# A list scheduler that chooses its plan by replays with varied times, in a fused fp32 attention, channel-mix and state-space kernel

## The chip, the cores and the metric

The kernel runs on one core of a Trainium2 chip, in float32 throughout. The metric is the device time of one execution in microseconds: the median over the runs of one kernel. A core has five engines with instruction queues of their own: TensorE (PE in the profile, its weight loads PEld), VectorE (DVE), ScalarE (ACT), GpSimd (POOL) and SyncE (SP), which here only issues transfers. Each works through its queue in order, and an instruction that waits for another engine holds up everything behind it in its own queue. So the order in which a program is written out, engine by engine, decides what waits for what.

## The reference

The input is X, 4 batches of 1024 tokens of 256 features. Four layers follow one another, each adding its result to x; LN is a layer norm over the features without weights.

```python
x = x + attention(LN(x))          # causal, one head of 256: softmax(Q K^T / 16) V
x = x + mix(LN(x))                # channel mix
x = x + states(LN(x))             # state space, 16 states
x = x + mix(LN(x))                # channel mix, the same weights

def mix(x):
    x_prev = shift(x, 1)          # the token before, 0 for the first
    xr = mu_r * x + (1 - mu_r) * x_prev
    xk = mu_k * x + (1 - mu_k) * x_prev
    return sigmoid(xr @ W_r.T) * (relu(xk @ W_k.T) ** 2 @ W_v.T)

def states(x):                    # has a layer norm of its own, with ln_g and ln_b
    x_proj, z = split((LN(x) * ln_g + ln_b) @ W_in.T + b_in)
    B_proj = x_proj @ W_B.T * mean(dt)
    y = causal_convolution(B_proj, mean over d of A_bar ** t) @ W_C.T + D_skip * x_proj
    return (y * silu(z)) @ W_out.T + b_out + x
```

The output is the last x.

## The kernel before

x stays in SBUF, 32 tiles of 128 tokens (eight to a batch). Work goes by half batches of 512 tokens, numbered 0 to 7; most operations on VectorE, ScalarE and GpSimd are 128 partitions by 512 floats. Operands of TensorE with the features on the partitions come from the rows by a detour through DRAM: normalised rows are written out (`.w`), read back in blocks (`.r0` to `.r3`), and turned by VectorE within 32 by 32 blocks (L731).

Every piece of work has a name, and the prediction uses these. The letter in front is the layer: `a` attention, `f` the first channel mix, `h`, `s`, `z` and `y` the state layer, `g` the second channel mix; then the half batch. `a6.st0` to `st3` are the statistics of the four tiles of half batch 6 (L603 and L604, VectorE), `.ve`, `.rs`, `.mrs` the small powers and shifts (L629, L642 on GpSimd, L651), `.xn0` to `.xn3` the normalised rows (L657 on VectorE or L663 on ScalarE), `a6.xa0` and `a6.xa1` the turned columns. `a1.q1` is a copy of queries out of PSUM. For a batch `qs2`, `qs3` are the query products, done in the manner of Strassen and Winograd with seven products `p1` to `p7` of blocks in place of eight: `T1` to `T4` are sums of inputs (L813), `u1` a copy out of PSUM, `u2`, `u3`, `c11` to `c22`, `v12` sums of outputs (L838). `gks0` to `gks3` and `zs0` to `zs3` do the same for the second mix's keys and the state layer's gates. `p22` is the masked maximum of tile 22's scores with its copy out of PSUM (L1502 and L1508), `v23` tile 23's values (L1474), `pT` a turned probability block (L1550), `a.x18` the addition of tile 18's attention into x. In a mix `xr0`, `xr1`, `xk0`, `xk1` are the mixed operands (L927 on ScalarE, L930 on VectorE), `pr0`, `pr1` the gate products into PSUM (L881), `g0`, `g1` their sigmoid (L1016), `relu`, `ka` the keys (L987 and L988), `pv` the value products, `rv` their product with the gate (L1038, VectorE), `x0`, `x1` the addition into x (L1044, GpSimd). `y0.6` and the like multiply z with the state layer's output (L1903), `pyo` are that layer's output products.

No scheduler of the language orders this program: it is scheduled by hand, by the class `Order`. While the kernel is described, `op` logs an operation with its needs and one or several ways to do it (an engine and an assumed time; an engine written as `DVE+port` shares a port with GpSimd), `unit` logs a group of matmuls, whose order on TensorE is that of the description, and `take` and `known` log a PSUM tile taken and a time given. PSUM is two pools, four tiles `bank` and two `pair`; a group takes the tile that came free first, by the model.

`finish` then plans. `_due` gives each operation a time at which it must be done for TensorE never to wait. For each of 20 plans, `_run` simulates the program: when an engine is free it takes, among the operations that could start within WAIT of the first, the one due soonest; a way is chosen by its modelled end; SHARE and MARGIN hold an operation back by a part of its slack. Each plan is run five times (ROUNDS): after each run the operations that a TensorE group waited for are made due earlier (`_hurry`), by the wait. The run with the lowest modelled end, with its due times, is run again, and this time writes the instructions. Assumed times are such as `dve(n)`, 0.02 + n/850 us, or 1.27 for an addition of 512 columns on GpSimd; a transfer lands at the queue's modelled end plus LANDING, 0.24.

Of the kernel before, what the change touches and what calls it, by code (L numbers as in the profile page):

```python
# [4 lines left out]

# [47 lines left out]
class Order:  # L53
# [23 lines left out]
        for share, margin in ((0.2, 2.5), (0.1, 1.5), (0.3, 4.0), (0.2, 1.5), (0.1, 2.5))  # L77
        for wait in (0.0, 0.08, 0.15, 0.22)
    ]
    ROUNDS = 5  # L80
    TRIALS = 4
    BANKS = {"bank": 4, "pair": 2}
# [95 lines left out]
    def finish(self):  # L178
        dues = self._due()
        self.made = {e["key"]: n for n, e in enumerate(self.log) if e["key"] is not None}  # L180
        self.ends = []
        best = math.inf
        for plan in self.PLANS:
            self.due = list(dues)
            for k in range(self.ROUNDS):
                used = list(self.due)
                end = self._run(plan, False)
                self.ends.append((end, k, plan))
                if end < best:
                    best, chosen = end, (plan, used)  # L190
                for key, wait in self.waits:
                    self._hurry(key, wait)
        plan, self.due = chosen
        self._run(plan, True)

    def _hurry(self, key, wait):

        n = self.made[key]
        while self.log[n]["kind"] == "op":
            self.due[n] -= wait  # L200
            needs = self.log[n]["needs"]
            if not needs:
                return
            n = self.made[max(needs, key=lambda k: self.ready[k])]

    def _run(self, plan, emits):
        self.SHARE, self.MARGIN, self.WAIT = plan
        self.emits = emits
        self.waits = []
        self.now = self.at = 0.0  # L210
        self.free, self.ready, self.offered = {}, {}, []
        self.queue = self.port = 0.0
        self.waiting = {}
        self.psum = {kind: [0.0] * k for kind, k in self.BANKS.items()}
        for n, e in enumerate(self.log):
            if e["kind"] == "op":
                self._enter(n)
            elif e["kind"] == "known":
                self._done(e["key"], e["time"])
            elif e["kind"] == "take":  # L220
                heapq.heappop(self.psum[e["takes"]])
            else:
                self._unit(e)
        while self.offered:
            self._step()
        return max(self.now, *self.free.values())
# [57 lines left out]
    def _step(self):  # L284
        self.at, k = self._first()
        time, n = self.offered.pop(k)
        e = self.log[n]
        end, _, engine, emit = self._way(time, n)
        engine, _, port = engine.partition("+")
        self.free[engine] = end  # L290
        if port or engine == "POOL":
            self.port = end
        if self.emits:
            emit()
        if e["frees"]:
            heapq.heappush(self.psum[e["frees"]], end + self.LAG)
        if e["moves"]:
            for k, work in enumerate(e["moves"]):
                issued = end - (len(e["moves"]) - 1 - k) * self.log[n]["cost"] / len(e["moves"])
                self.queue = max(self.queue, issued + self.FLIGHT) + work  # L300
            self._done(e["key"], self.queue + self.LANDING)
        else:
            self._done(e["key"], end + e["lag"])
# [46 lines left out]
def hybrid_kernel(  # L350
# [548 lines left out]
    class Mix:  # L899
# [1329 lines left out]
```

## Time and profile before

| what | value |
|---|---|
| time of the runs | 465.42 us median (465.42, 465.47, 465.42) |
| the profiled execution's own time | 465.0 us |
| its span | 463.1 us |
| TensorE busy | 456.0 us, 98% of the span |
| VectorE busy | 390.2 us, 84% |
| ScalarE busy | 220.8 us, 48% |
| GpSimd busy | 143.1 us, 31% |
| share of the last-ending chain | PE 86%, DVE 8%, issue 2%, DMA, POOL and ACT 1% each |
| HBM traffic | 149 GB/s over the span |

The span runs from the first to the last recorded instruction of the profiled execution; 1.9 us of that execution lie outside it. A row of a timeline is: start, length in us, engine, line, operation, output and input, number of instructions joined in the row; in brackets, the idle time of that engine before it and what ended it. Rows of one engine may overlap a little, since the next instruction begins while the last one ends. L numbers are lines of the kernel before.

### The profile page before, as it was taken

The page shows a single profiled execution, that of the slowest core. Times are in us where ns is not written, and L with a number is a line of the kernel's source. Part 1 is how long each engine was busy: PE and PEld are TensorE (multiplying, and loading weights), DVE is VectorE, ACT ScalarE, POOL GpSimd, SP SyncE. Part 2 cuts the span into 40 slices and gives each one's busy share as a digit, 9 for nine tenths or more (in the row PEclk, how much of TensorE's full clock was granted, in tenths as well). Part 3 has the DMA queues.
Part 4 walks back from the last instruction along what each step waited for, and adds up shares of the span by engine and source line. Part 5 has one row for each costly group of instructions (what it writes and reads, how often), then busy time and mean ns, then how long its engine had stood idle before and what let it go on. Part 6 is the DMA issues. An engine that isn't in the chain of part 4 may idle for free.

```text
span 463.1 us, 6634 instructions
## 1 busy us (share of the span) xinstructions
PE 456.0 (98%) x2052; PEld 312.5 (67%) x2052; DVE 390.2 (84%) x931; ACT 220.8 (48%) x463; POOL 143.1 (31%) x149
## 2 busy tenths in 40 slices
PE   8999999999999999999999999999999999999996
PEld 5766785667786667786777775474565758675875
DVE  3687769899969999889999977459889999999962
ACT  3422414454342433333556567441458777664652
POOL 3000102112013213121271354962052616826340
PEclk9999999999999999999999999999999999999999
DMA  8047876848455763427866989603022024252442
GB/s 242 21 127 203 250 190 168 222 132 258 117 135 139 221 194 93 118 62 237 224 177 182 275 268 271 260 17 88 11 92 91 1 86 144 81 147 99 129 144 84
DMA packets 84915, 69.44 MB, mean 150 GB/s; under 512 B 20160, under 2 KB 82576, under 8 KB 84880
## 3 DMA queue, kind: packets, MB, share of 16 engines
q1 hardware_dynamic: 84064, 68.76, 50.8%
q10 hardware_dynamic: 816, 0.26, 0.2%
q8 instruction: 16, 0.26, 0.2%
q14 instruction: 19, 0.16, 0.1%
HBM read 40.54 MB, written 28.45 MB: 149 GB/s over the span
## 4 chain that ended last, share of the span: by engine, by line
PE 86%; DVE 8%; issue 2%; DMA 1%; POOL 1%; ACT 1%; SPq 0%; DVEq 0%; POOLq 0%
PE po L1597 13%; PE sc L1492 13%; PE pv L1464 5%; PE p_zs L830 4%; PE p_ss L830 4%; PE p_qs L830 2%; PE p_gks L830 2%; PE py L1848 2%; PE pc L1798 2%; PE dust L1282 1%; DMA blocks_a<-rows_a 1%; PE pr_g0.pr L881 1%; PE pb L1735 1%; PE pp_a0.pq L774 1%; PE pr_g0.pv L881 1%
## 5 line engine op out<-in xcount | busy, mean ns | idle before, releaser
L1597 PE MATMUL po<-v,prT 128*128 128x256 f32 x288 | 67.7, 380 | 0.1
L1492 PE MATMUL sc<-xa,q 128*128 128x512 f32 (+3 forms) x192 | 67.0, 486 | 0.0
L1597 PEld LDWEIGHTS po<-v,prT 128*128 128x128 f32 x288 | 54.2, 189 | 11.6 <-issue 2.6
L1513 ACT ACTIVATE pr<-pr,nmx 128x128 f32<-128x128 f32 (+7 forms) x32 | 24.7, 773 | 64.6 <-DVE pr L1508 57.7
L1492 PEld LDWEIGHTS sc<-xa,q 128*128 128x128 f32 x192 | 35.1, 190 | 24.5 <-issue 19.6
L1464 PE MATMUL pv<-wv,xa 128*128 128x257 f32 x128 | 32.9, 380 | 0.0
L642 POOL TENSOR_TENSOR rs_a<-ve_a,minus_half 128x4 f32<-128x4 f32 x7 | 7.1, 1010 | 76.8 <-DVE ve_a L629 76.8
L1044 POOL TENSOR_TENSOR x<-x,r_f 128x512 f32<-128x512 f32 x16 | 20.3, 1271 | 33.0 <-DVE r_f L1038 32.5
L642 POOL TENSOR_TENSOR rs_h<-ve_h,minus_half 128x8 f32<-128x8 f32 x8 | 13.2, 1647 | 52.5 <-DVE ve_h L631 52.5
L1464 PEld LDWEIGHTS pv<-wv,xa 128*128 128x128 f32 x128 | 23.6, 191 | 7.8 <-issue 3.6
L1508 DVE TENSOR_SCALAR_CACHE_REDUCE pr<-sc,v 128x128 f32<-128x128 f32 (+7 forms) x32 | 26.2, 818 | 1.1
L1550 DVE STREAM_TRANSPOSE prT<-pblocks 128x384 f32<-128x384 f32 (+7 forms) x30 | 23.8, 793 | 2.4 <-DMA pblocks<-exps 2.3
L642 POOL TENSOR_TENSOR rs_f<-ve_f,minus_half 128x4 f32<-128x4 f32 x8 | 8.4, 1053 | 47.1 <-DVE ve_f L629 28.8
L1044 POOL TENSOR_TENSOR x<-x,r_g 128x512 f32<-128x512 f32 x14 | 18.9, 1371 | 11.0 <-DVE r_g L1038 11.0
L1641 POOL TENSOR_TENSOR x<-x,bout_r 128x512 f32<-128x512 f32 x16 | 20.0, 1279 | 4.5 <-ACT x L1634 4.5
L1606 DVE SCALAR_TENSOR_TENSOR x<-po,rsm,x 128x256 f32<-128x256 f32 x32 | 15.0, 470 | 4.3 <-PE po L1597 3.8
L1474 DVE TENSOR_TENSOR v<-pv,bv_r 128x257 f32<-128x257 f32 x32 | 13.4, 418 | 5.6 <-PE pv L1464 5.6
L930 DVE SCALAR_TENSOR_TENSOR xr_g<-hT_g,mur,xr_g 128x512 f32<-128x512 f32 x16 | 17.3, 1112 | 0.0
L663 ACT ACTIVATE xn_f<-x,mrs_f,rs_f 128x256 f32<-128x256 f32 x18 | 9.8, 592 | 15.5 <-DVE mrs_f L651 15.5
L1634 ACT ACTIVATE x<-x,mrs_h,rs 128x256 f32<-128x256 f32 x32 | 16.9, 592 | 0.0
L1903 POOL TENSOR_TENSOR z<-z,skip 128x512 f32<-128x512 f32 x9 | 13.1, 1462 | 10.9 <-DVE skip L1899 10.7
L663 ACT ACTIVATE xn_g<-x,mrs_g,rs_g 128x256 f32<-128x256 f32 x23 | 12.4, 589 | 8.3 <-DVE mrs_g L626 6.7
(458 smaller groups left out, 1089.8 us busy)
## 6 DMA issues: line engine op xcount, KB each, us to landing
hk<-r_dram SPq DMA_DIRECT2D x16, 512.0 KB, 9.2
rows_g<-xn_g SPq DMA_DIRECT2D x8, 512.0 KB, 2.9
blocks_g<-rows_g SPq DMA_DIRECT2D x32, 128.0 KB, 2.8
x<-in_L_attn_a_X_dram SPq DMA_DIRECT2D x7, 512.0 KB, 4.9
rows_f<-xn_f SPq DMA_DIRECT2D x7, 512.0 KB, 3.0
blocks_f<-rows_f SPq DMA_DIRECT2D x28, 128.0 KB, 2.7
rows_h<-xn_h SPq DMA_DIRECT2D x7, 512.0 KB, 3.7
blocks_h<-rows_h SPq DMA_DIRECT2D x28, 128.0 KB, 3.2
```

The lines of the kernel that those rows point to most:

```text
L642: nc.gpsimd.tensor_tensor(rs()[:, :k].rearrange("p k n -> p (k n)"), ve()[:, :k].rearrange("p k n -> p (k n)"), minus_half[:, : k * NH], A ...
L663: nc.scalar.activation(place(n), split(row(n)), AF.Identity, bias=mrs()[:, k - 1, n : n + 1], scale=rs()[:, k - 1, n : n + 1],)
L830: lambda: nc.tensor.matmul(p(), lhsT=w(), rhs=data(), start=True, stop=True), "bank",
L930: nc.vector.scalar_tensor_tensor(t()[:, c, :], hT()[:, c, :HALF], mu1[:, c : c + 1], t()[:, c, :], ALU.mult, ALU.add,)
L1044: nc.gpsimd.tensor_add(xg, xg, r()[:, ts(g, 2), :])
L1464: nc.tensor.matmul(pv()[:, : D + 1], lhsT=xaj()[:, c, ts(n, P)], rhs=wv[:, c, :], start=(c == 0), stop=(c == KC - 1),)
L1492: nc.tensor.matmul(sc()[:, k * HALF : k * HALF + w], lhsT=qh()[:, c, ts(n, P)], rhs=keys[k]()[:, c, :w], start=(c == 0), stop=(c == KC - 1),)
L1508: nc.vector.tensor_scalar(dst, src, v[2 * b + h]()[:, n, D : D + 1], None, ALU.add, ALU.min, accum_out=nmx(),)
L1513: nc.scalar.activation(p()[:, :nk], p()[:, :nk], AF.Exp, bias=nmx(), scale=-1.0, accum_out=sm())
L1550: nc.vector.transpose(dst()[:, : NH * width].rearrange("p (k m a) -> p k m a", m=NH, a=GRP), blocks().rearrange("p m (k a) -> p k m a", a= ...
L1597: nc.tensor.matmul(po()[:, :D], lhsT=src()[:, ts(n, P)], rhs=v[2 * b + n // NH]()[:, n % NH, :D], start=(n == 0), stop=(n == t),)
L1641: nc.gpsimd.tensor_add(xg, xg, bout_r.unsqueeze(1).to_broadcast([P, 2, D]))
```

## The change

`finish` still runs all plans and rounds, but judges each run by `_replays`, the mean end of six replays. A replay goes through the order that the run recorded in `self.trail`, with the engines it chose, and keeps both. Operation times are stretched at random, VectorE's by up to 3%, ScalarE's by up to 4%, GpSimd's by up to 25%, and a transfer lands up to 0.6 us later; TensorE's times stay. What is hurried for the next round is also new: in place of what TensorE waited for in the run, it is what TensorE waited for in the replays, by the mean wait, if that is over 0.1 us. No operation, no assumed time and no arithmetic is edited. The chosen plan and due times differ, and with them the order on each engine, the engine of some operations, and the PSUM tiles.

```diff
@@ class Order
+    SAMPLES = 6
+    SPREAD = {"DVE": 0.03, "ACT": 0.04, "POOL": 0.25}
+    LATE = 0.6
@@ finish
                 used = list(self.due)
-                end = self._run(plan, False)
+                self._run(plan, False)
+                end = self._replays()
                 self.ends.append((end, k, plan))
@@
+    def _replays(self):
+        lost, ends = {}, 0.0
+        for k in range(self.SAMPLES):
+            rng = random.Random(k)
+            ends += self._replay(rng, lost)
+        self.waits = [(key, t / self.SAMPLES) for key, t in lost.items() if t > 0.1 * self.SAMPLES]
+        return ends / self.SAMPLES
+
+    def _replay(self, rng, lost):
+        now = queue = port = 0.0
+        free, ready = {}, {}
+        psum = {kind: [0.0] * k for kind, k in self.BANKS.items()}
+        for n, way in self.trail:
+            e = self.log[n]
...
+            if e["kind"] == "unit":
+                for _ in range(e["many"] if e["takes"] else 0):
+                    at = max(at, heapq.heappop(psum[e["takes"]]))
+                if last is not None and at > now + 0.1:
+                    lost[last] = lost.get(last, 0.0) + at - now
+                now = max(now, at) + e["cost"]
+                ready[e["key"]] = now + self.LAG
+                continue
+            engine, shared, cost = way
+            if e["moves"]:
+                at = max(at, queue - self.FLIGHT - 0.5)
+            at = max(at, free.get(engine, 0.0), port if shared or engine == "POOL" else 0.0)
+            spread = self.SPREAD.get(engine, 0.0)
+            at += cost * (1.0 + spread * rng.random())
+            free[engine] = at
+            if shared or engine == "POOL":
+                port = at
...
+            if e["moves"]:
+                for k, work in enumerate(e["moves"]):
+                    issued = at - (len(e["moves"]) - 1 - k) * e["cost"] / len(e["moves"])
+                    queue = max(queue, issued + self.FLIGHT) + work
+                at = queue + self.LANDING + self.LATE * rng.random()
...
+        return max(now, *free.values())
@@ _run
-        self.waits = []
+        self.waits, self.trail = [], []
@@ _step
-        end, _, engine, emit = self._way(time, n)
+        end, start, engine, emit = self._way(time, n)
         engine, _, port = engine.partition("+")
+        self.trail.append((n, (engine, port, end - start)))
```

More of the change, by code (lines that the diff above doesn't have):

```diff
@@ L2 @@
 import math
+import random
 from contextlib import ExitStack
@@ L194, in finish @@
         self._run(plan, True)
+    def _replays(self):
[11 more added lines that the diff above has]
+            e = self.log[n]
+            if e["kind"] == "known":
+                ready[e["key"]] = e["time"]
+                continue
+            if e["kind"] == "take":
+                heapq.heappop(psum[e["takes"]])
+                continue
+            last, at = None, 0.0
+            for k in e["needs"]:
+                if ready[k] > at:
+                    last, at = k, ready[k]
+            if e["kind"] == "unit":
[5 more added lines that the diff above has]
+                ready[e["key"]] = now + self.LAG
+                continue
+            engine, shared, cost = way
[7 more added lines that the diff above has]
+                port = at
+            if e["frees"]:
+                heapq.heappush(psum[e["frees"]], at + self.LAG)
+            if e["moves"]:
[3 more added lines that the diff above has]
+                at = queue + self.LANDING + self.LATE * rng.random()
+            else:
+                at += e["lag"]
+            if e["key"] is not None:
+                ready[e["key"]] = at
+        return max(now, *free.values())
     def _hurry(self, key, wait):
@@ L218, in _run @@
             elif e["kind"] == "known":
+                self.trail.append((n, None))
                 self._done(e["key"], e["time"])
             elif e["kind"] == "take":
+                self.trail.append((n, None))
                 heapq.heappop(self.psum[e["takes"]])
@@ L223, in _run @@
                 self._unit(e)
+                self.trail.append((n, None))
         while self.offered:
```

## The prediction

> **What bounds the kernel now.** I read the page first, then the table of 20 us windows, then TensorE's list of waits, then the timeline around each wait.
>
> ```profile
> PE 456.0 (98%) x2052; PEld 312.5 (67%) x2052; DVE 390.2 (84%) x931; ACT 220.8 (48%) x463; POOL 143.1 (31%) x149
> ```
>
> TensorE works 456.0 of 463.1 us. Its order and its instructions are the same after the change, and the granted clock is 1.000, so the 456.0 stay. What can move is the other 7.1 us. The windows (columns: the stretch, its length, busy us of PE, weight loads, DVE, ACT, POOL, then clock, DMA share and GB/s) say where they lie:
>
> ```profile
> 0.00:20.00 20.00, 18.49 (x78) 11.90 (x79) 10.20 (x41) 7.64 (x16) 4.75 (x18) 1.00 0.51 151
> ...
> 140.00:160.00 20.00, 20.00 (x73) 13.12 (x72) 19.04 (x59) 6.92 (x14) 5.52 (x5) 1.00 0.66 182
> ...
> 380.00:400.00 20.00, 19.31 (x92) 15.81 (x91) 18.50 (x33) 13.60 (x33) 12.50 (x11) 1.00 0.34 105
> 400.00:420.00 20.00, 20.00 (x80) 14.80 (x79) 19.48 (x33) 13.29 (x23) 9.66 (x9) 1.00 0.48 145
> 420.00:440.00 20.00, 19.02 (x71) 13.23 (x71) 19.25 (x34) 11.08 (x19) 9.46 (x9) 1.00 0.37 119
> 440.00:460.00 20.00, 19.36 (x81) 14.54 (x79) 10.15 (x20) 9.74 (x16) 5.10 (x5) 1.00 0.38 119
> ```
>
> 1.5 us go at the start, about 4 after the last matmul. Between lie two gaps, 0.69 in 380 to 400 and 0.98 in 420 to 440, and scraps (0.06, 0.11, 0.02). In the list of TensorE's waits (us in total, times, longest) the first row is the start:
>
> ```profile
> PE dust L1282 <- DVE idle L427: 1.2, 1, 1.2
> PE p_gks L830 <- DVE u_gks L765: 1.0, 1, 1.0
> PE pr_g2.pr L881 <- ACT r_g L1016: 0.7, 1, 0.7
> PE pp_a0.pq L774 <- DVE xa L765: 0.3, 1, 0.3
> ```
>
> Measured from start to start of matmuls (a run of x2 against its usual pitch) the two gaps cost 1.15 and 0.85 us, and one at 92.9 costs 0.22. A perfect order of the other engines wins these, some 2.2 us, and no more. What it can lose is larger: VectorE is busy 19.04 of 20 in 140 to 160 and 19.25 to 19.48 from 400 on, so what is put before a needed operation there delays it by its whole length.
>
> **The change.** It picks another plan, (0.1, 2.5, 0.15) in place of (0.1, 2.5, 0.22), with other due times. I set the instructions of both programs side by side by engine. TensorE's groups keep their order, 66 operations change engine, 40 of 326 PSUM tiles follow another tile in their bank. Seven leave GpSimd (gks0.T3, y0.6, y1.7, gks1.T1, gks1.T3, gks2.T4 to VectorE, f0.ka0 to ScalarE), three join it (qs2.T1, qs2.T4, y0.4), the rest are halves swapped between VectorE and ScalarE. The transfers are the same ones, 399 and 3. I cost each place by its needs.
>
> *Start, 0 to 60 us.* Small halves change engines (a0.xa0 and a0.xa1, a1's xn, a1.q1, a3.q1). The nearest later group is fed with 0.25 us to spare. Nothing, plus or minus 0.1; without that cover the 0.75 us of a1.q1's row would show.
>
> *qs2's first product, 92.9 us.* It needs a4.xa1 and a4.xa0:
>
> ```profile
> 91.53 1.30 DVE L731 STREAM_TRANSPOSE xa<-blocks_a 128x512 f32<-128x512 f32 x2 [1.03 <-DMA blocks_a<-rows_a]
> ...
> 92.89 1.12 PE L830 MATMUL p_qs<-xa,wq 128*128 128x512 f32 x2
> ```
>
> After the change f0.relu1 (+0.65) and f1.st0 (+0.61) stand ahead of them. 1.03 us of idle time absorbs most; but SP issues the reads of tile 11's probability blocks before a4's, and f1.st3 is behind a.x10 too. I put the pair at 93.3 instead of 92.83: stall 0.7 instead of 0.22, so +0.45 (bounds 0 and +0.9).
>
> *qs3's first product, 158.9 us: the main loss.*
>
> ```profile
> 156.82 1.30 DVE L731 STREAM_TRANSPOSE xa<-blocks_a 128x512 f32<-128x512 f32 x2
> ...
> 158.86 1.02 PE L830 MATMUL p_qs<-xa,wq 128*128 128x512 f32 x2
> ```
>
> Before, a6.xa1 and a6.xa0 end at 158.13, 0.73 ahead. Afterwards p22 (1.47 with its accumulator read, its own row at 161.76), h1.st1 and h1.st0 (0.61 each) stand ahead of them: 2.69. One normalising pass net moves from VectorE to ScalarE (two a6.xn leave, one comes): −0.33, and v23 stays behind. In three-us windows VectorE is busy 2.96, 3.00, 2.93, 2.74, 2.67 from 144 to 159, 0.70 us short of full, and of that I let half be filled before the pair. 158.13 + 2.69 − 0.33 − 0.35 = 160.1 against 158.8 wanted: TensorE comes 1.3 us late (bounds 0.6 and 1.7: all 0.70 us of idle used and 0.35 off for the overlap of some 25 rows, or no idle used). This absorbs the delay at 92.9, for the lateness does not add: the operands come at a time, not after a wait. Behind it are queued f2's gates and the next scores, all fed over 1 us early until 255. Total by 160: +1.3.
>
> *160 to 360 us.* h5's transposes go behind h7's, y0.0 and y1.1 move, pyo0.4 takes another bank. TensorE's groups there keep over 0.5 us but for two, which get 0.05 to 0.1: +0.1. VectorE's idle time (8 us in 280 to 300) is the cover.
>
> *The gap at 395.7.* The second half of g2's gate waits for the sigmoid of the first to free the PSUM tile:
>
> ```profile
> 393.10 1.89 PE L881 MATMUL pr_g2.pr<-w_r,xr_g 128*128 128x256 f32 x8
> ...
> 395.03 0.60 ACT L1016 ACTIVATE r_g<-pr_g2.pr 128x512 f32<-128x512 f32 x1 [1.16 <-PE pr_g2.pr L881]
> ...
> 395.68 1.56 PE L881 MATMUL pr_g2.pr<-w_r,xr_g 128*128 128x256 f32 x6 [0.69 <-ACT r_g L1016]
> ```
>
> Afterwards it takes the bank that g1.rv1 on VectorE (393.66 to 394.33 before) freed. If VectorE is on time, −0.85.
>
> *The gap at 425.5.*
>
> ```profile
> 424.66 0.68 DVE L765 COPY u_gks<-p_gks 128x512 f32<-128x512 f32 x1
> ...
> 425.48 1.10 PE L830 MATMUL p_gks<-T_gks,w_fk 128*128 128x512 f32 x2 [0.98 <-DVE u_gks L765]
> ```
>
> The copy goes to ScalarE, idle then, and is done at about 423.3: −1.15 at best. What decides is VectorE. From 356 to gks2.c11 it gets six products (6 x 0.61 = 3.66), g3.xn0 (0.33) and four statistics of g7 (2.44), and loses y0.4, g1.ka1, g3.ka1, the copy (2.44) and four xn (1.33): +2.66. Against it stand its 2.15 us of idle time from 376 to 424, and stretching: while GpSimd works, some of VectorE's SBUF operations take longer.
>
> ```profile
> 387.60 2.43 DVE L930 SCALAR_TENSOR_TENSOR xr_g<-hT_g,mur,xr_g 128x512 f32<-128x512 f32 x2
> ...
> 387.77 1.71 POOL L1903 TENSOR_TENSOR z<-z,skip 128x512 f32<-128x512 f32 x1 [0.31 <-DVE skip L1899]
> ```
>
> Two such operations take 1.40 without it (394.85), so y1.7 cost VectorE 1.0 to 1.1 us. The Trainium skill, "SBUF — State Buffer", section on the two separate sides, says that VectorE with two SBUF inputs and a GpSimd operation exclude each other for the whole instruction. By it each of the five late products taken off GpSimd would give VectorE back its length (1.27, 1.71, 1.27, 1.27, 1.61): 7.1, more than the 2.66, and both gaps close, −2.0. By the rows only three or four operations are stretched, by 1.1 each (xr_g here, mrs_g and xn_g of 422.06 and 423.23, mrs_g near 398.5), 3.3 to 4.4, and the remaining GpSimd work may meet others in their place. I take the rows, and half of the stretches as moved elsewhere: 1.9 back, and of the 2.15 us of idle half is usable, so 2.66 − 1.9 − 1.1 = −0.3. gks2.c11 then comes at about 425.1 instead of 425.4; behind it g6.xn1, g5.ka0 and two xn of g7 join (0.33 + 0.61 + 0.66), so g6.xk0 ends near 437.3 instead of 436.2, and its group wants it at 438.5. Both gaps would close then; about half is taken off for waits that I can't place on an engine that is over 95% full: late gain −0.9 (bounds −2.0 and +0.5).
>
> *Sum.* +1.3 + 0.1 − 0.9 = +0.5. On the profiled execution, 463.1 of span and 1.9 around it: 465.5. It stands 0.4 below the median of the runs, so the forecast is 465.42 + 0.5 = 465.9.
>
> **The rivals.** 0.2%, 0.93 us, is about what a measurement of this kernel can tell from no change.
>
> A, the sum above: 465.9, its own range 465.0 to 466.8. Chance 0.45.
>
> B, faster: both late gaps close (−2.0) because the stretches really go with the products, and of the early loss half is hidden, as ScalarE (6.92 busy of 20) and an earlier start of the a6 reads help: −2.0 + 0.65 = −1.35, 464.1. For it: 1.15 and 0.85 are the only large gaps, and both direct causes are removed. Against it: p22 is 1.47 us and has no cover. Chance 0.18.
>
> C, slower: VectorE becomes the bound between 376 and 440. If only one of four stretches vanishes, +2.66 − 1.1 − 0.6 is +1.0 at gks2.T2, which feeds TensorE at 422.62, and nothing behind makes it up, since VectorE is full until 440. The late gain then is +0.5 and the whole +1.3 + 0.1 + 0.5 = +1.9: 467.3. It decides once the stretches give back less than about 1.5 us. For it: 19.48 of 20. Against it: of GpSimd's 33.0 us there five products, 7.1 us, leave. Chance 0.27.
>
> D, nothing in effect: the early loss is hidden by the queue's slack and only one gap closes or reopens elsewhere, 465.3. Chance 0.10.
>
> **How the numbers follow.** Likeliest A, 465.9. About half of B lies below 464.2 and a third of C above 467.8, together 0.18; the range leaves these out. Faster by over 0.93 (below 464.49): most of B and a little of A, 0.19. Slower (above 466.35): all but a little of C and a third of A, 0.40. Within: 0.41.
>
> **What would show it.** TensorE's waits should name xa L731 at p_qs near 159 with 0.9 to 1.5 us, and the rows pr_g2.pr and u_gks should be gone. VectorE's busy time should hardly change, GpSimd's fall by some 6 us. xr_g's longest should fall from 1.8 to 0.75. The prediction is wrong if qs3's wait is under 0.4 (then the SP order or the shifted start covers p22), or if new waits on T_gks or xk_g appear after 400 (then C).

## The result, and the profile after

| | before | after |
|---|---|---|
| median of the runs (8 each) | 465.37 us | 467.26 us |
| lowest to highest | 464.16 to 465.69 | 466.57 to 468.65 |
| the profiled execution, its span | 465.0, 463.1 us | 466.57, 464.8 us |
| TensorE, VectorE, GpSimd busy | 456.0, 390.2, 143.1 us | 455.3, 391.3, 141.3 us |

The ratio of the times is 1.0053, 95% interval 1.0040 to 1.0066: the changed kernel is 0.5% slower, by 1.9 us between the medians and 2.5 by the ratio. The prediction said 465.9, no difference that can be measured, with 0.40 for slower. The time lies inside the range of 464.2 to 467.8 and almost at the rival C (467.3), but the likeliest case was wrong.

TensorE's list of waits in the kernel after (us in total, times, longest; its lines are 65 higher than before):

```profile
PE p_qs L895 <- DVE xa L796: 2.8, 2, 2.4
PE dust L1347 <- DVE idle L492: 1.2, 1, 1.2
PE pr_g3.pv L946 <- ACT ka_g L1053: 0.9, 1, 0.9
PE p_gks L895 <- DVE ka_g L903: 0.6, 1, 0.6
```

The two old rows, pr_g2.pr and u_gks, are gone, as forecast, and the expected row on xa stands on top. But it is 2.4 us long, not 1.3, and two new late rows of 0.9 and 0.6 have come in. They are on ka_g, not on T_gks or xk_g, which the prediction named as the sign of rival C. The windows (columns as before) place them:

```profile
140.00:160.00 20.00, 18.17 (x65) 11.56 (x63) 18.25 (x57) 8.24 (x17) 5.94 (x5) 1.00 0.70 179
160.00:180.00 20.00, 19.39 (x80) 12.56 (x81) 19.72 (x43) 10.90 (x20) 9.98 (x12) 1.00 0.56 168
...
380.00:400.00 20.00, 20.00 (x96) 16.73 (x96) 19.36 (x33) 15.06 (x34) 9.36 (x9) 1.00 0.31 101
400.00:420.00 20.00, 19.04 (x73) 13.21 (x72) 19.03 (x38) 13.67 (x23) 9.15 (x7) 1.00 0.44 137
420.00:440.00 20.00, 19.45 (x76) 13.88 (x74) 18.70 (x36) 10.13 (x17) 7.97 (x8) 1.00 0.38 124
```

140 to 160 was full before; now 1.83 us are missing there and 0.61 in the next row. 380 to 400 has become full, 400 to 420 has lost 0.96.

TensorE's instructions are the same 2052 in the same order, so the two traces can be subtracted instruction by instruction. The table gives the start of a group in both and, in the last column, how much the lag of the kernel after grew since the row above.

| group | before | after | after minus before | growth |
|---|---|---|---|---|
| first query product, pp_a0.pq | 12.84 | 11.69 | −1.15 | −1.15 |
| qs2.p1 | 92.89 | 92.08 | −0.81 | +0.34 |
| qs3.p1 | 158.86 | 160.61 | +1.75 | +2.56 |
| po of tile 20 | 176.82 | 178.60 | +1.77 | 0 |
| g0.pr1 | 358.44 | 360.22 | +1.78 | 0 |
| g2.pr1 | 395.68 | 395.97 | +0.29 | −1.49 |
| g3.pv1 | 414.43 | 416.12 | +1.69 | +1.40 |
| gks2.p4 | 425.48 | 426.13 | +0.65 | −1.04 |
| gks2.p5 | 426.42 | 427.70 | +1.29 | +0.64 |
| g6.pk0 | 438.49 | 440.08 | +1.59 | +0.30 |
| last matmul | 459.09 | 460.75 | +1.67 | +0.08 |

Of the first row 0.17 us is the change's: TensorE waits 0.12 us before its first query product, where it waited 0.29, and so it does in each kernel below with the start of the one or the other. The rest, about 1 us, is not the change's. TensorE begins at half pace (the first x8 row below takes 0.43 us for each product), and in the profiled execution of before it stays so until 7 us, in that of after until about 5:

```profile
1.19 3.59 PE L1282 MATMUL dust<-idle 128*128 128x512 bf16 x8 [1.19 <-DVE idle L427]
4.74 1.09 PE L1293 MATMUL pt_wq_n<-ident,wq 128*128 128x128 f32 x4
5.62 1.06 PE L1282 MATMUL dust<-idle 128*128 128x512 bf16 x2
```

```profile
1.19 3.60 PE L1347 MATMUL dust<-idle 128*128 128x512 bf16 x8 [1.19 <-DVE idle L492]
4.79 0.80 PE L1358 MATMUL pt_wq_n<-ident,wq 128*128 128x128 f32 x4
5.43 0.59 PE L1347 MATMUL dust<-idle 128*128 128x512 bf16 x2
```

In the kernels below the first query product begins anywhere between 11.4 and 12.9 us, and by over 1 us apart where the start is the same (11.44 in u_p22, 12.48 in u_a7). So I count from that product: to po of tile 20 it takes 163.98 us before and 166.91 after (+2.93), to the last matmul 446.25 and 449.06 (+2.81). The early part loses 2.9 us (0.17 less with what the start wins), and the late part wins 0.1. u_same, the same order run again, gives 449.06 too.

### The profile page after: what moved, and what is told of

Its sections match the earlier page's. It is cut to its first block, busy times and chain, and to the rows that moved or that the text cites. A ratio compares the mean times of both kernels' runs of the same rounds, so it can differ in the third digit from the quotient of the medians.

```text
span 464.8 us, 6655 instructions
## 1 busy us (share of the span) xinstructions
PE 455.3 (98%) x2052; PEld 312.1 (67%) x2052; DVE 391.3 (84%) x935; ACT 221.4 (48%) x464; POOL 141.3 (30%) x145
## 4 chain that ended last, share of the span: by engine, by line
PE 78%; DVE 8%; DMA 6%; SPq 3%; ACT 2%; issue 2%; DVEq 0%; POOL 0%; ACTq 0%; POOLq 0%
PE po L1662 11%; PE sc L1557 9%; PE pv L1529 4%; PE p_zs L895 4%; PE p_ss L895 4%; PE p_qs L895 3%; PE p_gks L895 2%; DMA blocks_a<-rows_a 2%; PE py L1913 2%; PE pc L1863 2%; DMA rows_a<-xn_a 1%; SPq L790 1%; SPq L1610 1%; PE dust L1347 1%; DVE r_g L1103 1%
## 5 line engine op out<-in xcount | busy, mean ns | idle before, releaser
L1109 POOL TENSOR_TENSOR x<-x,r_f 128x512 f32<-128x512 f32 x16 | 21.3, 1333 | 21.9 <-DVE r_f L1103 13.2
L1109 POOL TENSOR_TENSOR x<-x,r_g 128x512 f32<-128x512 f32 x14 | 20.1, 1444 | 14.9 <-DVE r_g L1103 14.8
L728 ACT ACTIVATE xn_f<-x,mrs_f,rs_f 128x256 f32<-128x256 f32 x15 | 8.3, 592 | 21.0 <-DVE mrs_f L716 21.0
L707 POOL TENSOR_TENSOR rs_g<-ve_g,minus_half 128x4 f32<-128x4 f32 x8 | 9.0, 1124 | 24.8 <-DVE ve_g L686 14.9
L992 ACT ACTIVATE xk_f<-hT_f,muk 128x512 f32<-128x512 f32 x16 | 11.0, 715 | 9.9 <-DVE hT_f L796 9.7
```

What stands on the lines that cost most here:

```text
L707: nc.gpsimd.tensor_tensor(rs()[:, :k].rearrange("p k n -> p (k n)"), ve()[:, :k].rearrange("p k n -> p (k n)"), minus_half[:, : k * NH], A ...
L728: nc.scalar.activation(place(n), split(row(n)), AF.Identity, bias=mrs()[:, k - 1, n : n + 1], scale=rs()[:, k - 1, n : n + 1],)
L1109: nc.gpsimd.tensor_add(xg, xg, r()[:, ts(g, 2), :])
```

## The experiments

Fourteen of the sixteen kernels don't plan: the recorded order of the kernel before (b_) or after (u_) is written into the file as a list of operations with their engines, and `finish` emits it; then single entries are moved. With nothing moved (u_same) this gives the long waits of the kernel after again, 2.4, 0.8 and 0.6 us, with the lines of the kernel before. The other two (p_) keep the planner. Where only an order is edited, the diff shows that engine's order.

### Which of two waits is in front of qs3.p1

VectorE in the kernel after, ahead of the late product:

```profile
146.96 0.23 DVE L716 SCALAR_TENSOR_TENSOR mrs_a<-rs_a,mv_a 128x4 f32<-128x4 f32 x2
...
157.24 1.30 DVE L796 STREAM_TRANSPOSE xa<-blocks_a 128x512 f32<-128x512 f32 x2 [1.30 <-DMA blocks_a<-rows_a]
158.47 0.27 DVE L1567 TENSOR_TENSOR sc<-sc,mask 128x128 f32<-128x128 f32 x1
158.77 1.15 DVE L1573 TENSOR_SCALAR_CACHE_REDUCE pr<-sc,v 128x896 f32<-128x896 f32 x1
159.84 0.08 DVE L1573 DVE_READ_ACCUMULATOR pr<-sc,v 128x1 f32 x1
159.84 1.30 DVE L796 STREAM_TRANSPOSE xa<-blocks_a 128x512 f32<-128x512 f32 x2
```

The three rows of 158.47 to 159.84 are p22, the step that I had costed. But VectorE also stood idle for 1.30 us before 157.24, waiting for a7's blocks, on an engine that I had taken as nearly full. The reason is the first row: a7.mrs now stands behind a6.mrs (one row, x2), whose input GpSimd finishes at 146.62, while a7's own was there from 141.23 on. So a7's rows were normalised 3 us later than before (from 147.1 instead of 144.3). SyncE writes and reads both half batches behind each other:

```profile
148.23 1.02 SPq L784 DMA_DIRECT2D rows_a<-xn_a  x2
149.70 0.55 SPq L1604 DMA_DIRECT2D exps<-pr  x1
151.20 4.43 SPq L790 DMA_DIRECT2D blocks_a<-rows_a  x8
```

Before, the first write was issued at 145.38 and the last read by 154.4; here the first write is at 148.23 and the last read is issued by 155.6.

```diff
 u_p22, VectorE of the kernel after:
 h1.st1 h1.st0 a7.xa1 a7.xa0
-p22
 a6.xa0 a6.xa1
+p22
 v23 qs3.T1
```

> The order of the kernel after is written down and emitted as it is, but for one place: a6.xa0 and a6.xa1 stand ahead of p22 on VectorE. Theory 1 (the 2.6 us lost before qs3.p1 are two head-of-line waits in a row: 1.4 us of p22 ahead of a6.xa, and 1.2 to 1.3 us because a7's rows were normalised behind a6.mrs, so that a7's and a6's transfers landed late): TensorE's wait before qs3.p1 falls from 2.4 to 1.1 us, the time by 1.3 to about 466.0. Theory 2 (only what VectorE has to do ahead of a6.xa counts: p22 and two statistics): the same fall, 1.4. Theory 3 (VectorE is the bound later, so what is won at 160 us is lost after 400): the wait falls, the time stays within 0.4 of 467.3.

Measured: the wait is 1.1, the time 466.97 beside 464.75 for the kernel before on this chip, ratio 1.0048 (1.0031 to 1.0065): hardly less than the kernel after's. The place was found, yet a wait of 1.1 on r_f came up 19 us later.

```diff
 u_a7, VectorE:
 a6.st1 a.x16
+a7.mrs a7.xn0 a7.xn2 a7.xn3     (a7.xn1 keeps its place on ScalarE)
 pT0.18 a6.ve v21 rsm17 p20 a6.mrs
-a7.mrs a7.xn0 a7.xn2 a7.xn3
 SyncE:
 a7.w
+a7.r3
 a6.w
+a7.r2 a7.r1 a7.r0
 e20.w
-a7.r3 a7.r2 a7.r1 a7.r0
 a6.r3 a6.r0 a6.r2 a6.r1
```

(`e20.w` is the write of tile 20's probabilities.)

> The order of the kernel after, but a7.mrs and a7's four normalisations stand right behind a.x16 on VectorE and ScalarE, not behind a6.mrs, and SyncE issues a7's block reads ahead of and behind a6.w as the kernel before does, not behind the write of tile 20's probabilities. p22 stays ahead of a6.xa. Theory 1: the blocks of a7 and a6 land some 3 us and 1 us earlier, VectorE's 1.3 us idle before a7.xa goes, the wait before qs3.p1 falls from 2.4 to 1.1 to 1.2 us, the time to about 466.0. Theory 2: nothing changes, since the work ahead of a6.xa is the same: wait 2.4, 467.3. Theory 3: as theory 1 in the wait, the time within 0.4 of 467.3.

Measured: wait 1.5, VectorE's idle time before a7.xa 0.35 in place of 1.30, time 466.05, ratio 1.0025 (1.0013 to 1.0036). About half of the loss is gone, and no new wait came. Theory 2, on which my forecast rested, says that nothing changes here; it falls.

u_both is the kernel after with both edits.

> Both edits to the order of the kernel after. Theory 1: the two add up, the wait before qs3.p1 is under 0.2 us and the time 2.4 to 2.6 below that of the kernel after, 464.7 to 464.9; what is then left against the kernel before is the late part, about -0.3. Theory 2: wait 1.0, 465.9. Theory 3: wait under 0.2, but the time not under 466.5.

Measured: no wait on xa is left in the list; time 465.53, ratio 1.0019 (1.0012 to 1.0027). The two edits add up at qs3.p1 (2.32 us earlier against the lag before it). But the list of waits has a new row, and the timeline shows it:

```profile
175.38 0.65 PE L1199 MATMUL pb_all<-w_in,lnb_w 128*32 128x128 f32 x16
177.09 2.43 PE L1597 MATMUL po<-v,prT 128*128 128x256 f32 x10 [1.07 <-DVE r_f L1038]
```

In the kernel after this wait was hidden by the lateness. In the kernel before r_f was just in time, with nothing to spare:

```profile
176.12 0.65 DVE L1038 SCALAR_TENSOR_TENSOR r_f<-r_f,pr_f2.pv 128x512 f32<-128x512 f32 x1
176.82 1.16 PEld L1597 LDWEIGHTS po<-v,prT 128*128 128x128 f32 x6 [0.28 <-DVE r_f L1038]
```

VectorE is full on the whole stretch (19.72 of 20 in 160 to 180 in the kernel after), and the change had put statistics and shifts of h1 on it that the kernel before does later.

> The order of the kernel before, written down, with p22, h1.st1 and h1.st0 moved ahead of a6.xa1 and a6.xa0 on VectorE and nothing else: the very step that the prediction costed at +1.3, without the change's shift of a7's rows. The prediction's step: qs3.p1 comes 1.3 to 1.7 us later, 466.7 to 467.1. Theory 1, with a7's transfers as early as before and so no idle time of VectorE in front of a7.xa to take in the two statistics: all of 2.6 minus 0.73 of slack, +1.8 (467.2). Theory 3: a delay at 160 us is made up later, +0.5 at the most.

```diff
 b_p22, VectorE of the kernel before:
 h1.st3 h1.st2
+h1.st1 h1.st0 p22
 a6.xa1 a6.xa0 qs3.T1 v23 qs3.T2 qs3.T3 f3.mrs
-p22
 rsm19 pT1.20 qs3.c11 f3.xn3
-h1.st1
 (h1.st0 came 24 us later)
```

Measured: 466.96, ratio 1.0051 (1.0039 to 1.0063), the wait 1.5, and TensorE's lag grew by 1.66 at qs3.p1. (It also grew by 0.42 at h7's transposes, 288 us, but b_two and b_best below have 0.43 and 0.36 there without this edit.) The price of the step, forecast at 1.3, lies inside its bounds of 0.6 to 1.7. The change has a second cause beside it, and the two make up the whole: at the product itself the kernel after loses 2.60, this step alone gives 1.66, and u_a7, with the second cause gone, is left with 1.65.

Counted from the first query product, the four kernels and both originals line up (us to the end of f2.rv1 on VectorE, and to TensorE's last matmul):

| | f2.rv1 | last matmul | against before |
|---|---|---|---|
| before | 163.93 | 446.25 | |
| u_both | 164.90 | 447.13 | +0.9 |
| u_a7 | 165.36 | 447.71 | +1.5 |
| u_p22 | 165.92 | 448.19 | +1.9 |
| b_p22 | 165.79 | 448.54 | +2.3 |
| after | 166.79 | 449.06 | +2.8 |

The last column agrees within 0.3 us with the ratios of the timed runs (0.9, 1.2, 2.2, 2.4 and 2.5 us of 465).

### What the rest of the early loss is

Two kernels put h1's pieces back behind f2.rv1, on top of u_both.

```diff
 u_early, VectorE, on top of u_both:
-h1.st0 h1.ve h1.mrs
 ... f2.rv1
+h1.st0 h1.ve h1.mrs
 qs3.c12
 (GpSimd's h1.rs behind the shift of b_all, ScalarE's h1.xn0 behind f3.xkm0; h1.st1 stays)
```

> The order of the kernel after with both early edits (a7's rows first, a6.xa ahead of p22), and besides h1.st0, h1.ve, h1.rs, h1.mrs and h1.xn0 behind f2.rv1, no longer ahead of it. If it is these that make f2.rv1 late, some 1.0 us of VectorE, the wait of 1.07 on r_f at 177 us goes, and the time is 1.0 below that of u_both, at the kernel before's minus 0.3 to plus 0.2. If VectorE simply has too much to do there, the wait moves to the next operand and the time stays at 0.7 to 0.9 above the kernel before's.

Measured: 467.88, ratio 1.0072 (1.0050 to 1.0093). The wait on r_f fell only to 0.9, and my edit set up one of 1.7 on pv: h1.mrs, waiting for GpSimd, stood ahead of qs3.c12.

```diff
 u_early2, VectorE, on top of u_both:
-h1.st1 h1.st0
 a7.xa1 a7.xa0 a6.xa0 a6.xa1 p22 v23 ... f3.xn3
+h1.st1
-h1.ve
 ... f2.rv0 f4.ve
-h1.mrs
 ... f2.rv1 qs3.c12 w_in0 w_in1 rsm20 a.x20
+h1.st0 h1.ve
 p24 v25
+h1.mrs
 (ScalarE's h1.xn behind tile 24's exponents, GpSimd's h1.rs behind pv25)
```

> The order of the kernel after with both early edits, and h1.st1 back behind a6.xa and f3.xn3, h1.st0, h1.ve and h1.rs behind a.x20, h1.mrs behind v25, and ScalarE's four h1.xn behind e24, so that nothing of h1 stands where TensorE waits next. If the early loss is work moved ahead on a full VectorE, f2.rv1 comes 0.9 to 1.2 us earlier, the wait of 1.07 at 177 us goes without a new one over 0.5, and the time is that of the kernel before, minus 0.3 to plus 0.3. If it is the swaps as a whole, 0.6 to 1.0 above the kernel before's as in u_both.

Measured: 468.13, ratio 1.0070 (1.0055 to 1.0085), with waits of 0.8 on r_f, 0.7 on xa, 0.8 on b_all. Neither shows what makes r_f 1.0 us late in u_both (164.90 against 163.93); that stays open. What both show is that an edit by hand on this stretch costs two microseconds as easily as the planner's.

### The late part

```diff
 b_two, kernel before:
 VectorE: ... g0's skip product
+g1.rv1
 g3.xk1
-g1.rv1
 s6.x0
-VectorE: gks2.u1 behind g6.xn0
+ScalarE: gks2.u1 ahead of g6.xn1
```

> The order of the kernel before, written down, with the two late causes removed and nothing else: the copy gks2.u1 goes to ScalarE ahead of g6.xn1, and g1.rv1 stands one place earlier on VectorE, ahead of g3.xk1, by which g2.pr1 gets the PSUM tile that g1.rv1 frees. Theory A (the two gaps were local, so both are won in full): waits pr_g2.pr and u_gks gone, 1.9 to 2.0 us less, 462.8 beside 464.75. Theory B (VectorE is the bound from 376 on, so TensorE meets the next late operand): half of it at most, 463.8 or more, with new waits named on p_gks or pr_g3 after 395.

Measured: 464.53 beside 464.93, ratio 0.9988 (0.9977 to 0.9998). Both gaps close by 0.85 and 1.15 us at their places, and 0.59 comes back at 402.7, 0.94 at 407.0 (times of the kernel before). The list of waits says on what:

```profile
PE pr_g3.pr L881 <- DVE u_gks L838: 0.8, 1, 0.8
PE p_gks L830 <- DVE T_gks L813: 0.4, 1, 0.4
```

Theory B holds: of 2.0 us in two gaps that look local, 0.4 are won. It is the only version that beats both kernels, by 0.1%.

```diff
 b_prod, kernel before:
-y0.6, y1.7, gks1.T1, gks1.T3, gks2.T4 on GpSimd
+y0.6, y1.7, gks1.T1, gks1.T3, gks2.T4 on VectorE, in the same places
```

> The order of the kernel before, written down, with y0.6, y1.7, gks1.T1, gks1.T3 and gks2.T4 on VectorE at their places and nothing else: the disputed price of taking products off GpSimd. Theory A (the two engines exclude each other for the whole instruction): VectorE wins up to 7.1 us against 3.05 of added work, is early everywhere from 388 on, the wait on u_gks closes: 0.5 to 1.2 us less, about 463.8. Theory B (only three or four operations are stretched, by 1.1 each, and others are stretched in their place): VectorE's busy sum from 376 to 440 stays within 1 us of 61.1, the late waits stay or grow by up to 1 us: 464.6 to 465.8.

Measured: 468.54, ratio 1.0062 (1.0043 to 1.0080). Four of its six executions have a granted clock of 0.996, which the last section comes to; the profiled one has 1.000, took 466.57 us, and is 2.7 us behind the kernel before from the first query product on. This measures, in the order of the kernel before, the price that I had split between the skill's rule and the rows. Windows of b_prod, columns as before:

```profile
384.00:392.00 8.00, 8.00 (x39) 7.04 (x38) 8.00 (x12) 4.37 (x10) 3.52 (x3) 1.00 0.43 131
...
416.00:424.00 8.00, 6.86 (x28) 4.94 (x26) 8.00 (x9) 2.53 (x4) 7.37 (x6) 1.00 0.10 34
424.00:432.00 8.00, 6.90 (x21) 3.92 (x22) 7.69 (x14) 4.86 (x9) 0.26 (x1) 1.00 0.48 162
```

GpSimd's work from 376 to 440 fell from 33.0 to 25.4 us, VectorE's stayed at 61.3 (61.1). VectorE does only 9 instructions in 416 to 424, three of them stretched:

```profile
419.61 3.53 DVE L930 SCALAR_TENSOR_TENSOR xr_g<-hT_g,mur,xr_g 128x512 f32<-128x512 f32 x2
423.06 1.75 DVE L813 TENSOR_TENSOR T_gks<-xk_g,T_gks 128x512 f32<-128x512 f32 x1
```

Two xr_g take 1.40 when nothing disturbs them, the T_gks 0.68. Taking each instruction's length over the usual one of its own kind, five VectorE operations are stretched by 5.3 us together from 376 to 424 in the kernel before, and six by 5.4 in b_prod. Other operations took the places of those that were freed, so the five products brought VectorE their 3.05 us of work and gave nothing back, and TensorE waited 2.1 us for T_gks. The exclusion that the Trainium skill states ("SBUF — State Buffer", the two separate sides) fits a pair that meets: in the kernel before a stretched mrs_g ends at 399.76, the GpSimd product over it at 399.74. What doesn't follow is that fewer GpSimd instructions meet fewer VectorE instructions.

```diff
 u_all, on top of u_both:
-ScalarE: g3.ka1 behind g3.g1 and g5.xrm0
 VectorE: ... gks1.c12 g4.hT1 g5.hT0 gks1.c22
+VectorE: g3.ka1
 g4.xk0 g4.xr1 ... g7.st1 g7.st0
-VectorE: g6.mrs
 gks2.c11 gks2.u2
+VectorE: g6.mrs
 g6.xn1
```

> The order of the kernel after with the two early edits together (a7's rows first, a6.xa ahead of p22) and two late ones: g3.ka1 goes back to VectorE behind gks1.c22, and g6.mrs with the ScalarE rows that need it stands behind gks2.c11 and gks2.u2. Theory A: the two late waits of the kernel after (0.9 on ka_g before pr_g3.pv, 0.6 on ka_g before p_gks) go, and nothing takes their place: 465.5 minus 1.5, about 464.0. Theory B: VectorE is full there, the 0.61 us of g3.ka1 and the later g6.mrs come back as waits on xr_g, xk_g or xk of g6 before 440: 465.0 to 465.8.

Measured: 467.00, ratio 1.0035 (1.0022 to 1.0049). The lag at g3.pv1 shrank by 1.0, as expected of g3.ka1, and at gks2.p5 by 0.4; but 0.49 came back at gks2.p6, 0.77 at g5's gate, and 1.5 at g6.pk0, which waited 1.6 us for xk_g. Theory B again, and more than that.

```diff
 b_best, VectorE, on top of b_two:
-g6.st1 g6.st0 g6.st3 g6.st2 g6.ve     (seven other operations between them; g6.rs on GpSimd)
 ... gks1.v12 gks1.c12 gks1.c22
+g6.st1 g6.st0 g6.st3 g6.st2 g6.ve
 g4.hT1 g4.hT0 ... g3.rv0 g3.rv1
-g5.xr1 g5.xr0
 gks2.T2 gks2.T3 g6.mrs
-g6.xn0                                (to ScalarE, behind gks2.u1)
+g5.xr1 g5.xr0
 gks2.c11 gks2.u2
```

> The two late edits that closed the gaps of the kernel before, and besides VectorE cleared of what is not yet due: g6's four statistics, its ve and GpSimd's rs stand behind gks1.c22 instead of before gks1.T2, g5.xr1 and g5.xr0 behind g6.mrs instead of before gks2.T2, g6.xn0 goes to ScalarE. Theory B (VectorE's order decides what of a gap is won): the waits on T_gks at 402.9 and u_gks at 408.2 go, 1.0 to 1.8 us less than the kernel before, 463.1 to 463.9. Theory C (VectorE's amount of work decides, whatever its order): as before with new waits, 464.3 to 464.8.

Measured: 466.23, ratio 1.0021 (1.0011 to 1.0032). The waits of b_two were still there (0.8 and 0.4), and a new one of 1.3 before pr_g3.pv, on ScalarE's r_g. Moving what is not yet due out of the way won nothing; that it was moved in front of something that soon is due is my reading, not shown.

### Both parts apart, and both halves of the change apart

b_early takes the order of the kernel after up to f4's key products (215 us), then that of the kernel before; b_late the reverse:

```diff
 b_early:                                      b_late:
 order of the kernel after, to f4.pk0         -order of the kernel after, to f4.pk0
-order of the kernel after, from f4.pk0       +order of the kernel before, to f4.pk0
+order of the kernel before, from f4.pk0       order of the kernel after, from f4.pk0
```

(In both, the first part holds what the second order has emitted by f4.pk0.)

> Up to the key products of f4 (215 us) the operations stand in the order and on the engines of the kernel after, from there on as in the kernel before. Theory 1 (the loss is the early part, by the two waits before qs3.p1, and the late part wins a little): 1.9 to 2.5 us slower than the kernel before, 466.8 to 467.4, with waits of 2.4 us on xa at p_qs and the kernel before's own late waits of 0.7 and 1.0. Theory 2 (the loss is spread, the late part loses too): under 1.3 us slower.

Measured: 469.47 beside 465.25, ratio 1.0081 (1.0054 to 1.0108), more than the change itself; five of its six executions have a clock of 0.995 or 0.996. The wait before qs3.p1 is longer than in the kernel after, and behind it TensorE is slow:

```profile
161.78 1.58 PE L830 MATMUL p_qs<-xa,wq 128*128 128x512 f32 x2 [2.74 <-DVE xa L731]
163.15 3.17 PE L881 MATMUL pr_f2.pr<-w_r,xr_f 128*128 128x256 f32 x8
166.16 1.02 PE L830 MATMUL p_qs<-xa,wq 128*128 128x512 f32 x2
```

The same eight matmuls (`pr_f2.pr`) take 1.89 us in the kernel before. The windows of b_early give the granted clock (the third figure from the end) as 0.79 and 0.78 where it is 1.00 elsewhere:

```profile
160.00:164.00 4.00, 2.22 (x4) 1.28 (x5) 3.97 (x8) 1.72 (x3) 0.00 (x0) 0.79 0.33 97
164.00:168.00 4.00, 4.00 (x14) 2.98 (x13) 3.20 (x6) 1.57 (x3) 2.16 (x5) 0.78 0.69 215
```

So 1.8 us were lost behind the wait. From there to the end the lag stays within 0.3 (4.69 to 4.81): the late half behaves as in the kernel before.

> The counterpart: up to the key products of f4 as in the kernel before, from there on in the order and on the engines of the kernel after. Theory 1: 0 to 0.5 us faster than the kernel before, since two gaps (0.85 and 1.15) go and three waits (ka_g before pr_g3.pv, ka_g before p_gks, xk of g6) come back for some 1.7 of them. Theory 2: 0.6 us or more slower. The prediction's step said 0.9 faster.

Measured: 469.92, ratio 1.0109 (1.0090 to 1.0128). Inconclusive as a whole: the seam made waits of its own (1.8, 1.7 and 0.9 us between 224 and 265, on operands of f4, f5 and f7). Behind them the kernel after's own pattern repeats place by place (−0.85 at g2.pr1, +1.01 at g3.pv1, −1.15 at gks2.p4, +0.72 at gks2.p5), and from 265 to the end the lag goes from 5.1 to 4.9. So the late part is worth −0.2 us, with or without the early loss.

The change has two halves: the replays give a plan's time by which it is chosen, and they give the waits from which the next due times are made. p_judge takes the time alone from them, p_hurry the waits alone:

```diff
 p_judge:                                  p_hurry:
 self._run(plan, False)                   -self._run(plan, False)
+waits = self.waits                       +end = self._run(plan, False)
 end = self._replays()                    -end = self._replays()
+self.waits = waits                       +self._replays()
```

> One half of the change alone: plans are judged by the mean end of the replays, but what is hurried between rounds is still what TensorE waited for in the run itself. It picks plan (0.2, 1.5, 0.22). If judging by replays makes orders that are safer on the chip, the time is at or under the kernel before's, 464.0 to 464.8, with no wait of TensorE over 0.7 us. If the assumed times themselves are wrong at the places that matter (a head-of-line wait on VectorE, stretched operations), the sum of waits is as in the kernel after, 2 to 4 us, and the time 466 to 467.

> The other half of the change alone: what is hurried comes from the replays, but plans are judged by the end of the run itself. It picks plan (0.1, 1.5, 0.22). If the loss comes from judging by replays, this one is near the kernel before, 464.5 to 465.5. If any new draw of an order from these assumed times meets one or two waits that the times don't contain, it is 2 us or more slower, with single waits of 1 us and more on operands that VectorE makes.

Measured: 473.43, ratio 1.0178 (1.0160 to 1.0195), and 473.68, ratio 1.0184 (1.0152 to 1.0215). Either half alone is worse than both together. Their longest waits are all on what VectorE or ScalarE makes ready: 3.1 and 2.7 us on T_gks, 1.4 and 1.5 on xn_h, 1.9 on xn_f. (In each profiled execution TensorE also runs at half pace once, for 3.4 us, which costs up to 1.7.) Two more draws from the same assumed times came out 8 us slower, and the kernel after 2: the kernel before is a good draw, and in these three a criterion by replays did not improve it. Why the replays chose these orders was not tested.

### Does the wait also cost clock

The eight times of the kernel after go with the granted clock of their executions: 466.6 to 467.0 at 1.000, 467.0 and 467.5 at 0.998, 468.0 to 468.7 at 0.995. In u_dust eight products of a constant tile fill part of the wait:

```diff
+            def emit():
+                for _ in range(8 if (key, r) == ("qs3", 1) else 0):
+                    nc.tensor.matmul(p(), lhsT=idle[:, :P], rhs=idle, start=True, stop=True)
+                nc.tensor.matmul(p(), lhsT=w(), rhs=data(), start=True, stop=True)
```

> The order of the kernel after, written down and emitted as it is, for comparison on the same chip. Theory H (the wait of 2.4 us before qs3.p1 sets off a lower TensorE clock in part of the executions): granted clocks of 0.995 in about half of them, those 1.5 to 2 us longer than the ones at 1.000; median about 467.3, the fastest 466.5. Theory N (the clock is noise of the chip): the kernel before shows clocks of 0.995 as often.

> The same, but TensorE writes eight products of a constant bf16 tile (0.21 us each, 1.7 us) into qs3.p1's PSUM tile before the real product overwrites it, so that it works through most of its wait; nothing else moves, and qs3.p1 starts when it did. Theory H: no execution under 0.998, the long ones are gone, median 466.5 to 466.9, 0.4 to 0.9 below u_same. Theory N: the same spread and median as u_same. If the eight products delay qs3.p1, the time is up to 0.3 longer.

Measured: u_same 467.33, ratio 1.0055 (1.0035 to 1.0075), clocks 0.995 and 0.996 in two of seven executions, which are its two longest (468.2 and 468.6). u_dust 467.35, ratio 1.0049 (1.0031 to 1.0066), no clock under 0.999, and its longest execution 467.7. Of the kernel before beside them none of twelve is under 0.999, and of all its 104 executions beside the experiments one (0.995, 468.0 us). In u_p22, u_a7 and u_both (on another chip), whose waits at this place are 1.1, 1.5 and 0.1, none of 37 is under 0.998. So the lower clock goes with the long wait, as Theory H says. That filling the wait prevents it is not shown: none of six against five of fifteen can be chance. And the median did not fall. In the profiled execution of u_dust qs3.p1 starts within 0.1 us of where it did, but from 396 us on VectorE is 0.6 us later than in u_same, and TensorE waits 0.6 us for ka_g at 406.7; with single executions of both differing by 1.5 us the two medians can't be told apart. The lower clock explains the long executions of the kernel after, not its loss: the five others of the result have a median of 466.98, still 1.6 us above the kernel before.

## Why the prediction was wrong

*The bound and the method.* Right. Nothing but TensorE's waits differs, and the two old gaps closed by 0.85 and 1.15 as costed. VectorE's busy time hardly changed (390.2 to 391.3). GpSimd's products fell by 5.8 us, the forecast 6, but its other operations took some 4 us longer, so its busy time fell by only 1.8. The start, forecast at nothing, won 0.17.

*qs2's first product.* +0.45 was forecast, +0.34 measured. Single traces of kernels with nearly the same order differ by up to 1.3 us at this place (+0.1 to +1.0 in b_two and b_early against before), so it is not a size that one trace can give.

*qs3's first product, the step that failed.* I forecast +1.3, counted VectorE's queue ahead of a6.xa, and took the transfers as they were. Measured is +2.6 there, and +2.9 from the first query product to po of tile 20. The part costed (p22 and two statistics) was somewhat low, 1.66 in b_p22, though a statistic takes only 0.55 from start to start (154.77 to 155.32 in the kernel after), not 0.61. Missing was a second wait in the same queue, put at nothing: a7.mrs and a7's rows behind a6.mrs, which needs a later result of GpSimd. u_a7 shows it to be worth 1.0 us at qs3.p1 and 1.3 in time. It was in the order that I had before me: when I compared VectorE's two orders I priced what was moved ahead of the late operand, but not what was moved behind an instruction that is ready later, and not the write and the reads that hang on it.

*"All fed over 1 us early until 255."* Wrong: in the kernel before itself r_f ends at 176.77 and po of tile 20 starts at 176.82. Only TensorE's lateness hides this; u_both and u_p22 show a wait of 1.07 and 1.1 on r_f there, as soon as TensorE is less late at qs3.p1.

*Late gain, the second step that failed.* −0.9 forecast, −0.1 to −0.2 measured. Both gaps closed, and of the 2.0 us almost all came back at three places:

- +1.02 at g3.pv1, a cost that I had put at nothing. I took g3.ka1 off VectorE and didn't ask when ScalarE, behind gate and mix operations, would have it ready; TensorE waited 0.85 us for it. u_all, which puts it back on VectorE, is 1.0 better at this place.
- +0.71 at gks2.p5, which waits for what gks2.c11 frees. My own times held this wait: I put gks2.c11 at 425.1, so its end near 425.75, while a gap closed by 1.15 brings gks2.p5 from 426.42 to 425.27. I wrote that both gaps would close and didn't look at the next product.
- +0.23 at g6.pk0, the first product of g6's keys.

```profile
415.43 0.63 ACT L1053 ACTIVATE ka_g<-ka_g 128x512 f32<-128x512 f32 x1
416.12 3.29 PE L946 MATMUL pr_g3.pv<-w_fv,ka_g 128*128 128x256 f32 x14 [0.85 <-ACT ka_g L1053]
...
426.88 1.28 DVE L903 TENSOR_TENSOR ka_g<-p_gks,u_gks 128x512 f32<-128x512 f32 x2
```

The last row is gks2.c11 and gks2.u2; before, it began at 425.44. With TensorE 1.8 us later there, gks2.c11 is some 0.3 us earlier against it, as costed.

*The stretches.* xr_g's longest fell from 1.85 to 0.75, as forecast, but xk_g's rose from 0.80 to 1.77 and xr_f's from 0.75 to 1.77. From 376 us to gks2.c11 the stretches come to 5.3 us before and 4.0 after, so 1.3 came back where I had put 1.9; over the whole kernel it is 24 operations with 21.9 us before and 24 with 22.1 after. In b_prod nothing came back. The term was too high, but in the kernel after it is not what made TensorE wait for g3.ka1.

*Chances.* C had 0.27, and its 467.3 is almost the measured time, by luck: it put the late part at +0.5, which is a gain of 0.1 to 0.2, and the early part at +1.3, which is +2.9. The rule and the rows were both on the side of A. That a product taken off GpSimd gives something back, which they share, needn't hold: 1.3 of 1.9 came back late in the kernel after, nothing in b_prod and nothing over the whole kernel.

## What to carry to other kernels

On an engine that is over 95% busy, price a changed order by the whole queue: what is moved ahead of each operand, and what now stands behind an instruction that is ready later, with the transfers that hang on it. An operation that leaves for another engine has to be priced there too. A gap that looks local there is worth little (two gaps of 2.0 us gave 0.4 in b_two), since the same engine is late at the next operand; and work taken from a second engine that stretches the first can cost its full length (b_prod) unless the stretching is seen to go. A schedule that was chosen from many draws was not improved here by a criterion that looks wiser: compare its waits on the chip, not its modelled end.

## What the runs showed of the hardware

TensorE went to half pace behind a wait of 2.7 us in b_early (1.89 us of matmuls took 3.17). The two windows of 4 us with 0.79 and 0.78 make it 3.4 us at half pace, and 1.8 us were lost. In one execution of 465 us such a stretch gives a mean clock of 0.996, so I take the executions with 0.995 and 0.996 to have one each. In p_judge the pace halved at 292.4 us, behind waits of 0.5, 0.8 and 1.35 us with 0.7 us of matmuls between them, and not behind the single wait of 3.1 us at 430.6. After 2.4 us in the profiled execution of the kernel after it did not, while 5 of 15 timed executions of that order have a clock of 0.995 or 0.996. The Trainium skill, "TensorE: Matmul & The Clock Gate", section on the clock gate, says that the clock halves after an idle window of about 3.4 us that runs free of the kernel. The chance element agrees with the runs; the idle time is shorter here, 2.7 us in b_early. The start varies too: half pace lasts until 4.0 us in u_p22 and 7.2 in the kernel before, and the first query product begins at 11.4 and 12.8, 1.4 us of difference between two executions, of which 0.17 comes from the order.
